# Causal attention in a decoder kernel: the query-side mask moves from TensorE to VectorE

## The chip, the cores and the metric

The kernel runs on one core of one Trainium2 chip. The metric is the time of one execution on the device, in microseconds (us). The time given for a kernel is the median of its runs.

A core has five engines that run side by side, each with its own queue of instructions in order: TensorE (PE in the profile, its weight loads as PEld), VectorE (DVE, here also "the Vector"), ScalarE (ACT), GpSimd (POOL) and SyncE (SP, which here only starts DMAs). They wait for each other through semaphores. TensorE writes its results to PSUM, which here is used as eight banks of 512 float32 per partition; the other engines read them from there.

## The reference

The program is a decoder of four layers on `x` of 8 batches x 256 positions x 256 features. Each layer has a self-attention-like part, a cross-attention-like part and a feed-forward part. Of the twelve parts one has a causal mask, the self-attention of the last layer, and the change concerns only that one:

```
def _L3_attn_ref(x, Wq, bq, Wk, bk, Wv, bv, Wo, bo, Wq_lsr, Wk_lsr):
    N_HEADS = 16;  D_HEAD = 16;  LSR_RANK = 32          # x is (8, 256, 256)
    q = split_heads(x @ Wq.T + bq)
    k = split_heads(x @ Wk.T + bk)
    v = split_heads(x @ Wv.T + bv)
    q_lr = jnp.einsum('bhtd,hdr->bhtr', q, Wq_lsr)
    k_lr = jnp.einsum('bhtd,hdr->bhtr', k, Wk_lsr)
    scores = jnp.einsum('bhir,bhjr->bhij', q_lr, k_lr) / sqrt(LSR_RANK)
    causal_mask = jnp.triu(jnp.ones((Tq, Tq), dtype=bool), k=1)
    scores = jnp.where(causal_mask, -inf, scores)
    attn = softmax(scores, axis=-1)
    y = einsum('bhij,bhjd->bhid', attn, v)
    return merge_heads(y) @ Wo.T + bo
```

So there are 8 x 16 = 128 heads of 256 queries by 256 keys, each with 16 features.

## The kernel before

The parts run one after the other, and each has its own method. The causal part is `l3_attn` (L1708 to L1794). Its core is `attend` (L299), which the three cross-attention parts use too, without the mask.

**Two sets of scores.** A softmax over keys needs, for each query, the largest score to subtract. `attend` computes the scores twice. `score(n, t)` (L336) computes the scores of head n *by query*: partitions are 128 queries, t = 0 or 1 for the two halves, and keys lie along the row. `peak(n)` (L350) takes the negated maximum of each row on the Vector and writes it into one extra column of the query tile `q`. Later `turn` transposes that tile, so that the negated maximum becomes one more feature of the query. `weigh(m, k)` (L367) then computes the scores *by key*: partitions are 128 keys, queries lie along the row, and the extra feature (with a 1 on the key side) subtracts the maximum inside the matmul. `exponentials(m)` (L381) applies exp on ScalarE, and `blend` (L391) multiplies by the values. The by-key scores can be used as a matmul operand without a transpose.

**What the causal mask leaves.** Of the by-query scores the upper half of the queries needs 128 keys (t = 0), the lower half 256 (t = 1). Of the by-key scores the first 128 keys need 256 queries, the second 128 keys need 128. In each, two blocks of 128 x 128 lie on the diagonal, and there the triangle above the diagonal must get -1e30.

**The mask as a matmul.** `masked(bank, cols, which)` (L330) adds the triangle to both diagonal blocks of a bank with one matmul in bfloat16: weights are the identity, `self.tri[:, 0]`, and the moving operand is a triangle of 0 and -1e30, `self.tri[:, 1]` for scores by query and `self.tri[:, 2]` for scores by key (transposed), repeated twice. It accumulates onto the scores that are already in the bank, at line L334 in the profile. `peak` calls it ahead of its two `tensor_reduce` (L359), `exponentials` ahead of its exp (L388).

**The loop and its order.** The loop at L464 goes through slots n, one per head. In slot n it issues score(n, 0), weigh(n - 10, 0), score(n - 1, 1), weigh(n - 11, 1), then peak(n - 1) and exponentials(n - 11), and then whatever other work is due in this slot: projections and keys of the next batch, the transposes of `turn`, `divide` and `blend` after every fourth slot, the output projection, and the next part (`l3_xattn`), which is interleaved as `beside` and `behind`. The four score matmuls of a slot use 17 or 18 of the 128 rows of TensorE, each in another quarter of the rows, so that they can run at the same time; each float32 matmul is two instructions. The order of TensorE and of the Vector is the program's own order (`self.pinned = "both"`); ScalarE and GpSimd may be ordered by the planner. In the first ten slots there is no by-key work yet, in the last ten no by-query work.

**Banks.** Six PSUM banks (`ps_m`) go round between the scores by query, the scores by key and the other matmul results. A score bank becomes free when `peak` has read it, a by-key bank when exp has read it.

`tensor_tensor_reduce`, which the change brings in, already occurs once in this kernel, in the first layer: it shows in the profile as a pair of Vector instructions, `CUSTOM_DVE_ANT_0` (the elementwise operation and running reduction, which also writes its elementwise result, here to a tile that nobody reads) and `DVE_READ_ACCUMULATOR2_ANT` (which writes the reduced column).

Of the kernel before, what the change touches and what calls it, by code (L numbers as in the profile page):

```python
# [21 lines left out]
F32 = mybir.dt.float32  # L22
I32 = mybir.dt.int32
BF16 = mybir.dt.bfloat16
# [3 lines left out]
ALU = mybir.AluOpType  # L28
AX = mybir.AxisListType
PSUM = bass.MemoryType.PSUM  # L30

P = 128
B, S, D = 8, 256, 256
# [5 lines left out]
BIG = 1.0e30  # L39


C_COS, C_SIN, C_DECAY, C_CAUSAL, C_IOTA, C_PIDX, C_HEADS, C_ONE17, C_BEFORE, C_END = (
    0, 256, 512, 1024, 1280, 1536, 1538, 1666, 1667, 1795
)
# [18 lines left out]
class InOrder:  # L63


    def __init__(self, tc, engine):
        self.tc, self.engine = tc, engine
# [10 lines left out]
class Decoder:  # L78
    def __init__(self, ctx, tc, dram, out):
        self.tc, self.nc, self.dram, self.out = tc, tc.nc, dram, out  # L80
        nc = self.nc
        pool = lambda name, bufs, **kw: ctx.enter_context(tc.tile_pool(name=name, bufs=bufs, **kw))
        self.const = pool("const", 1)
        self.res = pool("res", 1)
        self.ring = pool("ring", RING)
        self.small = pool("small", 3)
        self.in_order = [InOrder(tc, e) for e in (nc.tensor, nc.vector, nc.scalar, nc.gpsimd)]
        self.flip = 0
        self.side = "left"

        self.pinned, self.next, self.ready = False, None, None

        self.x = []
        for b in range(B):
            xb = self.res.tile([P, 2, D], F32, tag=f"x{b}", name=f"x{b}")
            nc.sync.dma_start(xb, dram["x"][b].rearrange("(h p) d -> p h d", p=P))
            self.x.append(xb)
        self.xn = self.res.tile([P, NT, D], F32, tag="xn", name="xn")
        self.xnT = self.res.tile([P, 2, N], F32, tag="xnT", name="xnT")

        self.ident = self.const.tile([P, P], F32, tag="ident", name="ident")
        make_identity(nc, self.ident)
        self.ones = self.filled("ones", [P, P], 1.0)
        self.minus = self.filled("minus", [P, 2], -0.5)
        self.eps5 = self.filled("eps5", [P, 1], 1e-5)
        self.junk = self.const.tile([P, 512], F32, tag="junk", name="junk")
        self.cst = self.const.tile([P, C_END], F32, tag="cst", name="cst")
        nc.scalar.dma_start(self.cst, dram["consts"])

        self.tri = self.const.tile([P, 3, P], BF16, tag="tri", name="tri")  # L110
        nc.gpsimd.tensor_copy(self.tri[:, 0, :], self.ident)
        nc.gpsimd.tensor_copy(self.tri[:, 1:3, :].rearrange("p a s -> p (a s)"), self.cst[:, C_CAUSAL : C_CAUSAL + S])

# [183 lines left out]
    def attend(self, pool, nh, dh, prepare, finish, scale=1.0, causal=False, beside=None, behind=None):  # L299
# [14 lines left out]
        nc = self.nc  # L314
# [11 lines left out]
        def rows(n, k):  # L326
            h = n % nh
            return slice(R * (h % hp), R * (h % hp) + k), h // hp

        def masked(bank, cols, which):  # L330

            out = bank.rearrange("p (x s) -> p x s", s=P)[:, 0 : cols // P + 1 : cols // P, :]
            mask = self.tri[:, which : which + 1, :].to_broadcast([P, 2, P])
            self.pe(nc.tensor.matmul(out, lhsT=self.tri[:, 0, :], rhs=mask, start=False, stop=True))  # L334

        def score(n, t):  # L336

            if not 0 <= n < total:
                return
            q, kT, v = state[n // nh]  # L340
            if t == 0:
                ps[n] = self.bank(512)
            r, g = rows(n, dh + 1)
            w = P if causal and t == 0 else S
            self.pe(nc.tensor.matmul(  # L345
                ps[n][:, S * t : S * t + w], lhsT=qTs[n // hp][r, t * P : (t + 1) * P], rhs=kT[r, g, :w],
                start=t == 0 or not causal, stop=not causal,
            ))

        def peak(n):  # L350
            if not 0 <= n < total:
                return
            q = state[n // nh][0]
            to = q[:, :, n % nh, dh + 1]
            bank = ps.pop(n)
            if causal:
                masked(bank, 384, 1)
                for t, cols in ((0, slice(0, P)), (1, slice(S, 512))):
                    self.dve(nc.vector.tensor_reduce(  # L359
                        to[:, t : t + 1], bank[:, cols], axis=AX.X, op=ALU.max, negate=True  # L360
                    ))
            else:
                self.dve(nc.vector.tensor_reduce(  # L363
                    to, bank.rearrange("p (t s) -> p t s", t=2), axis=AX.X, op=ALU.max, negate=True
                ))
# [15 lines left out]
        def exponentials(m):  # L381
            if not 0 <= m < total:
                return
            bank = ps.pop((m, 1))
            if causal:
                masked(bank, 256, 2)
            p = pool.tile([P, n3], F32, tag="p", name="p", bufs=9 if halves else 5)
            nc.scalar.activation(p, bank[:, :n3], AF.Exp, scale=scale)  # L388
            live_p[m] = p
# [74 lines left out]
        while todo or now[0] <= total + lag + 1:  # L464
            n = now[0]
            m = n - lag
            if halves:
                score(n, 0), weigh(m, 0), score(n - 1, 1), weigh(m - 1, 1)
                peak(n - 1), exponentials(m - 1)
            else:  # L470
                score(n, 0), weigh(m, 0), score(n, 1), weigh(m, 1)
                peak(n), exponentials(m)
            for fn in todo.pop(n, ()):
                fn()
            now[0] += 1
# [1232 lines left out]
    def l3_attn(self, pool):  # L1708
# [3 lines left out]
        nc, dram = self.nc, self.dram  # L1712
        w = self.weights(dram["l3a_w"])
# [12 lines left out]
        a = pool.tile([P, 2, P], F32, tag="a", name="a", bufs=1)  # L1726
# [53 lines left out]
        def finish(b, o, later):  # L1780
# [9 lines left out]
            later(4, out)  # L1790
            return 6

        beside, behind = self.l3_xattn(pool)
        self.attend(pool, 16, 16, prepare, finish, 1.0 / math.sqrt(32.0), True, beside, behind)  # L1794

# [332 lines left out]
```

## Time and profile before

| | |
|---|---|
| median of 3 runs | 2464.55 us |
| the 3 runs | 2462.15, 2464.55, 2473.96 us |
| the profiled execution | 2461.47 us |
| its span, first to last instruction | 2459.7 us |
| mean granted TensorE clock over the span | 0.935 |
| the causal stage, from the start of the first mask matmul to that of the last | 2014.6 to 2316.0 us |
| mask matmuls in it (L334) | 256, half of them by query |
| `tensor_reduce` in it (L359) | 256, mean 352 ns |

The profile is one execution; its own time is 3.1 us below the median of the runs, so sums are made against it and then carried to the median. Busy time is given per engine and per group of instructions; the "granted clock" is the share of full speed that the chip's throttle gave to TensorE, 1.00 or 0.50 at any moment. The timeline lists instructions in order of time, with those of one kind that follow each other merged (x2 is two instructions, and the duration is that of both together), and in brackets the idle time ahead of an instruction with what ended it; "issue" there is time in which the engine waited for nothing that the profile shows. A table of windows gives busy time, number of instructions and granted clock of stretches of the span.

### The profile page before, as it was taken

To read this page: it belongs to the slowest core of one execution; us is meant where nothing else is said; L and a number is where in the kernel's file an instruction comes from. 1 tells how busy PE (TensorE), PEld (TensorE's weight loads), DVE (VectorE), ACT (ScalarE), POOL (GpSimd) and SP (SyncE) were. 2 spreads that over 40 slices of the span, in tenths; PEclk is the share of its full clock that TensorE was granted. 3 is DMA by queue.
4 is the path that set the end of the run, shared out by engine and by line. 5 is a ranking of instruction groups with operands and counts; after the bars stand their busy time and mean duration, and the time that the engine had idled before them with its cause. 6 is when DMAs were issued, how large, how long until landed. Compare 5 with 4: busy or idle time off the path is not lost. (4 is left out here: it accounts for less than half of the span.)

```text
span 2459.7 us, 31787 instructions
## 1 busy us (share of the span) xinstructions
PE 2217.8 (90%) x11611; PEld 1410.8 (57%) x11611; DVE 1245.0 (51%) x3192; ACT 872.7 (35%) x2118; POOL 501.0 (20%) x712
## 2 busy tenths in 40 slices
PE   7888889999999999899899955666999989999999
PEld 4555555666655555555568833444665555566556
DVE  5666553334323235676565558985453235555500
ACT  3433422334211113466113335664552114434311
POOL 3211333221000002221135534440222110000010
PEclk9999999999999999899899976886899998899999
DMA  3000000001100000121515643100111010000000
GB/s 128 1 1 1 30 14 26 18 10 41 52 13 26 13 18 13 48 66 36 210 53 165 153 95 104 46 18 14 49 39 32 1 52 10 18 18 18 3 13 22
DMA packets 56539, 103.68 MB, mean 42 GB/s; under 512 B 7624, under 2 KB 40224, under 8 KB 54720
## 3 DMA queue, kind: packets, MB, share of 16 engines
q1 hardware_dynamic: 44688, 75.90, 9.0%
q0 software_dynamic: 7680, 20.98, 3.7%
q10 hardware_dynamic: 4016, 4.76, 0.6%
q8 instruction: 94, 1.54, 0.3%
q14 instruction: 61, 0.50, 0.1%
HBM read 84.64 MB, written 16.78 MB: 41 GB/s over the span
## 5 line engine op out<-in xcount | busy, mean ns | idle before, releaser
L169 PE MATMUL mm<-xnT,w 128*128 128x512 f32 (+1 forms) x1104 | 475.3, 577 | 1.4 <-ACT xnT L252 0.7
L345 PE MATMUL mm<-kT,qT 17*128 17x256 f32 (+2 forms) x1536 | 322.4, 413 | 15.7 <-DVE q L363 12.7
L169 PEld LDWEIGHTS mm<-xnT,w 128*128 128x128 f32 x1104 | 210.6, 193 | 201.2 <-issue 192.1
L376 PE MATMUL mm<-qT,kT 18*128 18x256 f32 (+2 forms) x1536 | 309.5, 406 | 1.4 <-ACT p L388 1.2
L388 ACT ACTIVATE p<-mm 128x512 f32<-128x512 f32 (+1 forms) x384 | 212.1, 562 | 262.0 <-PE mm L376 137.1
L363 DVE TENSOR_REDUCE q<-mm 128x2 f32<-128x512 f32 x256 | 172.3, 688 | 164.1 <-PE mm L376 148.7
L345 PEld LDWEIGHTS mm<-kT,qT 17*128 17x128 f32 (+1 forms) x1536 | 179.1, 193 | 115.0 <-issue 41.3
L560 ACT ACTIVATE hT<-mm 128x512 f32<-128x512 f32 x104 | 62.1, 597 | 431.0 <-PE mm L169 416.6
L561 DVE TENSOR_TENSOR hT<-hT,mm 128x512 f32<-128x512 f32 x104 | 71.4, 687 | 278.2 <-PE mm L169 278.1
L536 PE MATMUL acc<-w,hT 128*128 128x256 f32 x832 | 195.5, 379 | 1.0 <-DVE x L271 1.0
L536 PEld LDWEIGHTS acc<-w,hT 128*128 128x128 f32 x832 | 157.9, 190 | 62.9 <-issue 41.6
L376 PEld LDWEIGHTS mm<-qT,kT 18*128 18x128 f32 (+1 forms) x1536 | 172.3, 191 | 13.2 <-issue 4.6
L235 POOL TENSOR_SCALAR rstd<-mv 128x2 f32<-128x2 f32 x64 | 12.3, 193 | 812.7 <-DVE mv L231 466.8
L399 PE MATMUL acc<-p,v 128*32 128x256 f32 (+2 forms) x1536 | 140.3, 386 | 0.0
L271 DVE TENSOR_TENSOR x<-x,mm 128x512 f32<-128x512 f32 x40 | 27.4, 686 | 193.1 <-PE mm L169 192.9
L297 ACT COPY qT<-tp 128x256 f32<-128x256 f32 x256 | 83.7, 375 | 84.0 <-PE tp L293 83.1
L1290 POOL DMA_INDIRECT xg<-xd,token x96 | 90.9, 947 | 87.8 <-PE tp L1413 54.2
L359 DVE TENSOR_REDUCE q<-mm 128x1 f32<-128x128 f32 (+1 forms) x256 | 78.7, 352 | 56.4 <-PE mm L334 56.1
L169 PE MATMUL mm<-wall,xT 128*128 x384 | 99.7, 383 | 1.1 <-DVE xT L1415 1.1
L293 PE MATMUL tp<-ident,q 128*128 128x128 f32 x512 | 90.6, 299 | 3.3 <-ACT qT L297 1.9
L399 PEld LDWEIGHTS acc<-p,v 128*32 128x32 f32 (+1 forms) x1536 | 61.1, 122 | 47.0 <-issue 21.5
L293 PEld LDWEIGHTS tp<-ident,q 128*128 128x128 f32 x512 | 60.7, 149 | 44.6 <-issue 32.0
(426 smaller groups left out, 3778.8 us busy)
## 6 DMA issues: line engine op xcount, KB each, us to landing
wall<-in_l1f_w SPq DMA_DIRECT2D x8, 1536.0 KB
yd<-y SPq DMA_DIRECT2D x96, 128.0 KB
kT<-in_ctxK SPq DMA_DIRECT2D x16, 512.0 KB
v<-in_ctxV SPq DMA_DIRECT2D x16, 512.0 KB
w<-in_l0f_w SPq DMA_DIRECT2D x8, 768.0 KB
cT<-in_ctxT SPq DMA_DIRECT2D x8, 512.0 KB
ctx<-in_ctx SPq DMA_DIRECT2D x8, 512.0 KB
w<-in_l2f_w SPq DMA_DIRECT2D x3, 768.0 KB
```

Source lines behind the costliest of these rows:

```text
L169: self.pe(self.nc.tensor.matmul(out, lhsT=lhsT, rhs=rhs, start=i == 0, stop=i == len(pairs) - 1))
L293: self.pe(self.nc.tensor.transpose(ps[:, i, t * P : (t + 1) * P], flat[:, t, g * P : (g + 1) * P], self.ident))
L297: self.nc.scalar.copy(dst, ps[:, i, :])
L345: self.pe(nc.tensor.matmul(ps[n][:, S * t : S * t + w], lhsT=qTs[n // hp][r, t * P : (t + 1) * P], rhs=kT[r, g, :w], start=t == 0 or not c ...
L359: self.dve(nc.vector.tensor_reduce(to[:, t : t + 1], bank[:, cols], axis=AX.X, op=ALU.max, negate=True))
L363: self.dve(nc.vector.tensor_reduce(to, bank.rearrange("p (t s) -> p t s", t=2), axis=AX.X, op=ALU.max, negate=True))
L376: self.pe(nc.tensor.matmul(ps[m, 1][:, 256 * k : 256 * k + w], lhsT=kT[r, g, k * P : (k + 1) * P], rhs=qTs[m // hp][r, S - w :], start=k = ...
L388: nc.scalar.activation(p, bank[:, :n3], AF.Exp, scale=scale)
L399: self.pe(nc.tensor.matmul(acc[r, S - w :], lhsT=v[:, k, (G * hp + i) % nh, :], rhs=live_p[G * hp + i][:, 256 * k : 256 * k + w], start=k ...
L536: self.pe(nc.tensor.matmul(acc[:, t, :], lhsT=hT[:, t * P : (t + 1) * P], rhs=units[i][2], start=i == 0 and t % 2 == 0, stop=i == len(unit ...
L561: nc.vector.tensor_tensor(hT, hT, u, ALU.mult)
L1290: (engine or self.nc.gpsimd).indirect_dma_start(out=dst, out_offset=None, in_=src, in_offset=bass.IndirectOffsetOnAxis(ap=rows, axis=0))
```

## The change

Scores by query are no longer masked on TensorE. `peak` instead calls `tensor_tensor_reduce` on the Vector for each half: it adds a tile `self.later` (0 for the first 128 keys where there are 256, then the triangle of 0 and -1e30) to the scores from PSUM, scales by -1, writes the result to a tile `self.void` that nobody reads, and takes the minimum along the row, starting from 1e30, which is the negated maximum. Scores by key keep their mask matmul, so `masked` loses its arguments and the triangle by query leaves `self.tri`. The score matmuls now each start and stop their own result (`start=True, stop=True`), since nothing is accumulated onto them. Two tiles of 1 KB per partition are set up once ahead of the part.

```
-        self.tri = self.const.tile([P, 3, P], BF16, tag="tri", name="tri")
+        self.tri = self.const.tile([P, 2, P], BF16, tag="tri", name="tri")
         nc.gpsimd.tensor_copy(self.tri[:, 0, :], self.ident)
-        nc.gpsimd.tensor_copy(self.tri[:, 1:3, :].rearrange("p a s -> p (a s)"), self.cst[:, C_CAUSAL : C_CAUSAL + S])
+        nc.gpsimd.tensor_copy(self.tri[:, 1, :], self.cst[:, C_CAUSAL + P : C_CAUSAL + S])
...
-        def masked(bank, cols, which):
+        def masked(bank):
-            out = bank.rearrange("p (x s) -> p x s", s=P)[:, 0 : cols // P + 1 : cols // P, :]
-            mask = self.tri[:, which : which + 1, :].to_broadcast([P, 2, P])
+            out = bank.rearrange("p (x s) -> p x s", s=P)[:, 0:3:2, :]
+            mask = self.tri[:, 1:2, :].to_broadcast([P, 2, P])
             self.pe(nc.tensor.matmul(out, lhsT=self.tri[:, 0, :], rhs=mask, start=False, stop=True))
...
-                start=t == 0 or not causal, stop=not causal,
+                start=True, stop=True,
...
             if causal:
-                masked(bank, 384, 1)
-                for t, cols in ((0, slice(0, P)), (1, slice(S, 512))):
-                    self.dve(nc.vector.tensor_reduce(
-                        to[:, t : t + 1], bank[:, cols], axis=AX.X, op=ALU.max, negate=True
-                    ))
+                for t, w in ((0, P), (1, S)):
+                    self.dve(nc.vector.tensor_tensor_reduce(
+                        out=self.void[:, :w], in0=bank[:, S * t : S * t + w], in1=self.later[:, S - w :], scale=-1.0,
+                        scalar=BIG, op0=ALU.add, op1=ALU.min, accum_out=to[:, t : t + 1],
+                    ))
...
-                masked(bank, 256, 2)
+                masked(bank)
...
+        self.void = pool.tile([P, S], F32, tag="void", name="void", bufs=1)
+        self.later = pool.tile([P, S], F32, tag="later", name="later", bufs=1)
+        nc.vector.memset(self.later[:, :P], 0.0)
+        nc.vector.tensor_copy(self.later[:, P:], self.cst[:, C_CAUSAL : C_CAUSAL + P])
         beside, behind = self.l3_xattn(pool)
         self.attend(pool, 16, 16, prepare, finish, 1.0 / math.sqrt(32.0), True, beside, behind)
```

## The prediction

> **What bounds the kernel now.** I read the page first, then the stage from the first mask matmul to the last (2014.4 to 2316.6) in the table of windows, then its groups of instructions by form.
>
> ```profile
> PE 2217.8 (90%) x11611; PEld 1410.8 (57%) x11611; DVE 1245.0 (51%) x3192; ACT 872.7 (35%) x2118; POOL 501.0 (20%) x712
> ...
> PEclk9999999999999999899899976886899998899999
> ```
> ```profile
> 2014.40:2316.60 302.20, 299.14 (x2421) 179.26 (x2422) 163.30 (x514) 122.38 (x293) 16.80 (x38) 0.95 0.05 15
> ```
>
> In the stage TensorE is busy 299.14 of 302.20 us, the Vector 163.30 (54%). The stage is as long as TensorE's queue. So what comes off that queue comes off the time, and work added to the Vector costs nothing until it delays TensorE. The clock is not full: 0.95 here, and two of the fortieths in the stage (2029 to 2152) show 8.
>
> ```profile
> L359 DVE TENSOR_REDUCE q<-mm 128x1 f32<-128x256 f32 x124 | 51.4, 415 | 0.0
> L334 PE MATMUL mm<-tri 128*128 128x256 bf16 x241 | 50.0, 289 | 0.0
> ...
> L359 DVE TENSOR_REDUCE q<-mm 128x1 f32<-128x128 f32 x124 | 35.9, 289 | 50.5 <-PE mm L334 50.3
> ```
>
> These groups (2020 to 2300) give a mask 289 ns, but matmuls overlap; what one adds to the queue is read from the timeline, a slot with both masks first, then one of the first ten, which has one:
>
> ```profile
> 2150.39 0.11 PEld L334 LDWEIGHTS <-tri 128*128 128x128 bf16 x2 [0.33 <-issue]
> ...
> 2150.72 0.18 PEld L345 LDWEIGHTS mm<-kT,qT 17*128 17x128 f32 x1 [0.21 <-issue]
> 2150.72 0.62 DVE L359 TENSOR_REDUCE q<-mm 128x1 f32<-128x128 f32 x2 [0.46 <-PE mm L334]
> ...
> 2151.05 0.37 PE L345 MATMUL mm<-kT,qT 17*128 17x256 f32 x1
> ...
> 2151.36 0.11 PEld L334 LDWEIGHTS <-tri 128*128 128x128 bf16 x2 [0.33 <-issue]
> ```
> ```profile
> 2017.20 0.10 PEld L334 LDWEIGHTS <-tri 128*128 128x128 bf16 x1 [0.33 <-issue]
> 2017.42 0.30 PEld L345 LDWEIGHTS mm<-kT,qT 17*128 17x128 f32 x4
> ```
>
> From the masks to the next score matmul it takes 2150.72 - 2150.39 = 0.33 us with two, 2017.42 - 2017.20 = 0.22 with one. A mask costs 0.107 us of the queue at full clock. The 0.33 us ahead of the masks stands in both cases, and stays as long as one mask is left.
>
> **The clock follows the work in the array.** The windows decide this case. Cutting the span into 3.41 us windows (the length of the shortest low stretch in the clock's record; all others are multiples), the clock is 1.00 or 0.50 for whole windows:
>
> ```profile
> 2098.11:2101.53 3.42, 3.25 (x31) 1.45 (x28) 2.76 (x9) 1.27 (x4) 0.89 (x2) 1.00 0.00 0
> 2101.53:2104.94 3.41, 3.41 (x16) 2.15 (x16) 1.61 (x6) 1.18 (x3) 0.00 (x0) 0.50 0.01 2
> ...
> 2255.13:2258.54 3.41, 3.24 (x39) 1.67 (x38) 3.06 (x10) 1.83 (x6) 0.88 (x2) 1.00 0.82 255
> 2258.54:2261.95 3.41, 3.41 (x36) 2.20 (x38) 2.75 (x10) 2.03 (x5) 0.00 (x0) 1.00 0.13 55
> ```
>
> Both first windows have TensorE busy 3.25 us; after one the clock is halved, after the other not. What differs is how much of the array works. I define a window's load as the sum over its matmul instructions of streaming time at full clock x rows x columns / (128 x 128), divided by 3.41 us. A float32 instruction streams 128 columns in 0.107 us (those of 512 columns follow each other after 0.43), a mask its 256 bfloat16 columns in 0.107. So a mask is 0.107 / 3.41 = 0.031. A slot's scores are eight instructions, 2 x (0.107 + 0.213 + 0.213 + 0.107) = 1.28 us, on 17.5 of 128 rows: 0.051. Four transposes are 0.125, a blend (32 of 128 columns) 0.19. The window from 2098.11 holds 2.6 slots and six masks: 0.32, low clock follows. That from 2255.13 holds a blend, two slots, 3.65 masks and a bit: 0.43, full clock follows. Over all 663 windows whose widths the trace gives, the load of a window told the clock of the next: below 0.375, half in 92 of 94; above, full in 568 of 569. TensorE's idle time is not what counts: the masks, full-array work, hold the clock up.
>
> **The change part by part.** *Masks by query, removed:* 128 x 0.107 = 13.7 us off the queue. In about four of the first ten slots no full-array work remains between two groups of scores, and the switch of up to 0.55 us goes too: at most 4 x 0.44 = 1.8 more, which I put at nothing, since these windows lose load as well.
>
> *The same masks, as load:* a stretch of slots alone, before, has a period of 0.96 us: 3.41 / 0.963 x (0.051 + 2 x 0.031) = 0.40, above 0.375. After, the period is 0.856: 3.41 / 0.856 x (0.051 + 0.031) = 0.33, below it. At half clock such a stretch is worth half, so the clock stays low until transposes, blends or projections fill a window. Taking the first mask of each pair out of the windows as they stand, those from 2070.81 (0.39 to 0.29), 2180.03 and 2255.13 (both 0.43 to 0.37) fall below, and four others come within 0.025; before there were three, from 2029.85, 2063.98 and 2098.11, with 9 low windows, 30.7 us, which cost half of that, 15.4. Where windows begin in the program is not fixed (the three runs spread over 12 us), so I moved the window border through 100 positions over TensorE's own order of the stage, low stretches brought to full speed, and applied the 0.375. Before: 2.3 falls, 33 us low, 16.6 lost. After, with 0.107 us taken out per mask: 6.8 falls, 87 us low, 43.5 lost; 49.4 if each slot also stalls 15 ns on the Vector. I take 46.5. Tenth and ninetieth per cent without stalls are 20 and 65. Against 16.6 that is +29.9, from +4 to +48.
>
> *Rule against row:* the Trainium skill, "TensorE: Matmul & The Clock Gate", section "HAM oscillation", says that the clock falls back when TensorE has idle gaps longer than about 3.4 us. In the low window from 2101.53, and in the one ahead of it, TensorE is busy 3.41 and 3.25 us. By that rule the clock term would be 0 and the sum -11.4 us; by the row it is +18.5.
>
> *Reductions become add-and-minimum:* the nearest rows are the same operation in the first layer:
>
> ```profile
> 63.36 0.43 DVE L71 CUSTOM_DVE_ANT_0 void<-e,u 128x256 f32<-128x256 f32 x1
> 63.71 0.08 DVE L71 DVE_READ_ACCUMULATOR2_ANT cm<- 128x1 f32 x1
> 63.91 0.16 DVE L71 SCALAR_TENSOR_TENSOR cb<-cm,ca 128x1 f32<-128x1 f32 x1
> ```
>
> 256 columns take 0.43 us, as the reduction does; the read starts 0.35 after and takes 0.08; the next starts 0.55 after, but needs the result. By the reductions 128 columns are 0.126 shorter. A pair is then 0.30 + 0.43 = 0.73 us, 0.62 if reads hide, 0.97 with 0.55 each; now 0.62. I take 0.73, the same operation without the dependence: 128 x 0.11 = 14 us (0 to 45) on the Vector, 54% to 59% busy. What hides it: the score matmul that ends last, from 2151.05 for 0.37, is done at 2151.42, 0.06 after the masks' start, so the pair starts at about 0.10 instead of 0.33. It ends at 0.83, at worst 1.07, and the bank is wanted back by the second next group, 0.22 + 0.86 = 1.08 after the masks (two slots of both before: 0.95 against 1.29). Behind it on the Vector wait only the later parts of the same slots. Cover is gone where the Vector is full already, 8.10 of 10 us from 2180 and 9.21 from 2280: about 8 slots x 0.11 each, 2 us together. At 0.97 it would be up to 128 x 0.11 = 14.
>
> *Setup and the rest:* a fill and a copy of 128 columns ahead of `l3_xattn` on the Vector: a 128x256 operation from SBUF is 0.29 us, so at most 0.6, while the Vector is busy 8.47 of 20 us there; 0.3. The shorter copy on GpSimd, `start`/`stop`, and the order of queues: nothing moves; 0.
>
> **Sum.** -13.7 + 29.9 + 2.3 = +18.5. From the median, 2464.55, that is 2483; from the profiled execution (2461.47, 15.4 lost), 2461.47 - 13.7 + 31.1 + 2.3 = 2481.2. Forecast 2482.
>
> **Rivals.**
> *The clock does not follow* (faster or the same): the load was only a companion of something else, perhaps of real idleness. Then -13.7 + 2.3: 2453, and 2451 with the first slots' switches; it decides if the falls stay at three. For it: l1_xattn runs slots without masks at 1.00 from 1019 to 1100. Against it: its score matmuls are all 256 wide and none of its windows there lies below 0.375; and the rule holds in 660 of 663.
> *Luck with the borders*: the batch's period falls from 37.8 us, about 11 windows, to 36, so borders drift through the batch; if only four falls come, at 43.5 / 6.8 = 6.4 us each, 26 are lost, 9 more than before: 2464.55 - 13.7 + 9 + 2.3 = 2462.
> *The Vector becomes the bound*: the pair costs 0.97, beyond the new slot's 0.856: +14 of stalls, which thin the load further (by 15 ns a slot the loss rose 6): 2464.55 - 13.7 + 14 + 33 = 2498. Against it: the 0.55 contains a wait for the result.
>
> **How the numbers follow.** The measurement can tell about 0.5%, 12.3 us. The forecast has 0.62 (0.50 of it beyond 2477, 0.12 below), the deaf clock 0.13 (0.06 below 2452, 0.07 within), luck 0.13 (0.02 below, 0.09 within, 0.02 beyond), the Vector 0.12. Faster 0.08, same 0.28, slower 0.64. The range goes from 2453, which leaves out most of the deaf clock's lower half, to 2499; within the forecast alone it is 2466 to 2497.
>
> **What would show it.** Masks at L334: 128 instead of 256, slots 0.107 us closer at full clock. Right: five or more falls of the clock in the stage, some 60 to 110 us at half clock (before 30.7), mean granted clock of the stage near 0.85, windows of slots alone at load 0.33 ahead of them. Vector pairs at 0.73 us, few TensorE waits for `q`. Wrong: slots closer and the clock at 0.95, or long TensorE waits for the Vector.

## The result, and the profile after

The changed kernel takes 2474.9 us, median of 13 runs (2469.57 to 2491.1), against 2465.78 for the kernel before in the same comparison (13 runs, 2459.58 to 2480.33). The ratio is 1.0041, 95% interval 1.0021 to 1.0061: slower by 10 us (5 to 15). The forecast was 2482 in a range of 2453 to 2499, so the sign and the range held; the loss is about half of what the sum said, and lies within the half per cent on which the prediction had put 0.28. In what follows one run, of the kernel called the addition alone, was in a slower state (2654.9 us, its others 2461 to 2477); it counts in that kernel's median and in no ratio.

The profiled execution took 2476.95 us, against 2461.47 before. Its page gives the engines' busy time and the granted clock in forty slices:

```profile
PE 2228.6 (90%) x11483; PEld 1413.5 (57%) x11483; DVE 1258.8 (51%) x3450; ACT 873.3 (35%) x2118; POOL 501.1 (20%) x712
...
PEclk9999999999999999899899977776999988887999
```

TensorE has 128 instructions fewer and is busy 10.8 us longer. In the second line the late run of 9s has turned into 8s and a 7: that is the causal stage. The table of windows for the stage, from the start of its first score matmul to that of its last mask (columns: window; its length, then busy time and instructions of TensorE, its weight loads, the Vector, ScalarE, GpSimd; granted clock; DMA share; GB/s):

```profile
2013.82:2332.59 318.77, 310.32 (x2293) 184.23 (x2292) 176.26 (x769) 123.13 (x293) 16.80 (x38) 0.87 0.05 14
```

The same stretch before:

```profile
2013.79:2316.00 302.21, 299.15 (x2421) 179.36 (x2420) 163.24 (x513) 122.25 (x293) 16.80 (x38) 0.95 0.05 15
```

The stage before took 302.21 us with TensorE idle for 3.06 of them and the clock at 0.95. After, it is 16.6 us longer, with 318.77 - 310.32 = 8.45 us idle, at 0.87. In the record of the clock the low stretches of the stage go from three (10.2, 3.4, 17.1 us; 30.7 together) to seven (13.7, 3.4, 3.4, 17.1, 17.1, 17.1, 13.7; 85.3 together). The execution as a whole is 15.5 us longer, so outside the stage it changed by -1.1.

The new Vector work, in the groups of instructions by form (2036 to 2316; busy us, mean ns, idle ahead):

```profile
L359 DVE CUSTOM_DVE_ANT_0 void<-mm,later 128x256 f32<-128x256 f32 x114 | 48.4, 425 | 4.0
...
L334 PE MATMUL mm<-tri 128*128 128x256 bf16 x114 | 35.3, 310 | 0.0
L359 DVE CUSTOM_DVE_ANT_0 void<-mm,later 128x128 f32<-128x128 f32 x114 | 32.8, 288 | 37.3 <-PE mm L345 32.5
...
L359 DVE DVE_READ_ACCUMULATOR2_ANT q<- 128x1 f32 x228 | 18.9, 83 | 0.0
```

and in the timeline, from one mask to the next, a slot without other work at full clock:

```profile
2163.00 0.10 PEld L334 LDWEIGHTS <-tri 128*128 128x128 bf16 x1 [0.33 <-issue]
...
2163.26 0.26 DVE L359 CUSTOM_DVE_ANT_0 void<-mm,later 128x128 f32<-128x128 f32 x1
...
2163.45 0.08 DVE L359 DVE_READ_ACCUMULATOR2_ANT q<- 128x1 f32 x1
...
2163.56 0.42 DVE L359 CUSTOM_DVE_ANT_0 void<-mm,later 128x256 f32<-128x256 f32 x1
...
2163.86 0.10 PEld L334 LDWEIGHTS <-tri 128*128 128x128 bf16 x1 [0.33 <-issue]
...
2163.91 0.08 DVE L359 DVE_READ_ACCUMULATOR2_ANT q<- 128x1 f32 x1
```

From one mask to the next it is 0.86 us, where it was 0.96 with two masks: the slot got shorter by what a mask costs. The Vector's pair goes from 2163.26 to 2163.99, 0.73 us. Both are as the prediction had them. The same view at half clock shows what a slot costs there:

```profile
2234.23 0.10 PEld L334 LDWEIGHTS <-tri 128*128 128x128 bf16 x1 [0.64 <-issue]
2235.72 0.10 PEld L334 LDWEIGHTS <-tri 128*128 128x128 bf16 x1 [0.64 <-issue]
```

That is 1.49 us, 1.74 times 0.854 (the median at full clock), not twice. Over 14 such slots the median is 1.487, so a microsecond at half clock loses 1 - 0.854 / 1.487 = 0.43 us; by the slots with two masks before, 1 - 0.962 / 1.700 = 0.43 as well. The prediction took 0.50.

Three windows of 3.41 us from the table of windows, the first two at full clock, the third following the second:

```profile
2142.51:2145.93 3.42, 3.25 (x42) 1.89 (x34) 3.25 (x13) 1.87 (x6) 0.88 (x2) 1.00 0.01 2
...
2224.43:2227.85 3.42, 3.25 (x35) 1.80 (x31) 3.25 (x13) 1.87 (x5) 0.88 (x2) 1.00 0.02 5
2227.85:2231.26 3.41, 3.41 (x17) 2.32 (x16) 2.40 (x14) 1.01 (x3) 0.00 (x0) 0.50 0.00 0
```

The first two have the same busy time on every engine to within a tenth, and TensorE is busy 3.25 us in both. By the load (streaming time x rows x columns of every matmul, worked out as in the prediction) the first is at 0.386 and the clock stays full after it; the second is at 0.341, and the third is at half clock.

### The profile page after: what moved, and what is told of

The parts are those of the page before. It is cut to its first block, busy times and chain, and to the rows that moved or that the text cites. A ratio compares the mean times of both kernels' runs of the same rounds, so it can differ in the third digit from the quotient of the medians.

```text
span 2474.0 us, 31852 instructions
## 1 busy us (share of the span) xinstructions
PE 2228.6 (90%) x11483; PEld 1413.5 (57%) x11483; DVE 1258.8 (51%) x3450; ACT 873.3 (35%) x2118; POOL 501.1 (20%) x712
## 5 line engine op out<-in xcount | busy, mean ns | idle before, releaser
L345 PE MATMUL mm<-kT,qT 17*128 17x256 f32 (+2 forms) x1536 | 331.8, 422 | 16.4 <-DVE q L364 12.7
L377 PE MATMUL mm<-qT,kT 18*128 18x256 f32 (+2 forms) x1536 | 318.4, 416 | 3.6 <-DVE q L359 2.1
L359 DVE CUSTOM_DVE_ANT_0 void<-mm,later 128x128 f32<-128x128 f32 (+1 forms) x256 | 91.2, 356 | 50.4 <-PE mm L345 40.6
```

Of the source, the lines that this page charges most:

```text
L345: self.pe(nc.tensor.matmul(ps[n][:, S * t : S * t + w], lhsT=qTs[n // hp][r, t * P : (t + 1) * P], rhs=kT[r, g, :w], start=True, stop=True,))
L359: self.dve(nc.vector.tensor_tensor_reduce(out=self.void[:, :w], in0=bank[:, S * t : S * t + w], in1=self.later[:, S - w :], scale=-1.0, sc ...
L377: self.pe(nc.tensor.matmul(ps[m, 1][:, 256 * k : 256 * k + w], lhsT=kT[r, g, k * P : (k + 1) * P], rhs=qTs[m // hp][r, S - w :], start=k = ...
```

## The experiments

Each was compared with the kernel before on the same chip, in three groups. The kernel before took 2462.03 us beside the first four (removal, addition, by-key scores over 32 rows), 2469.86 beside the four with whole groups of rows, and 2462.64 beside the other two, so only ratios are set against each other; a difference in us is the difference of ratios times the time of before. "Load theory" in the expectations is the prediction's: a window below a load of 0.375 is followed by half clock. A "fall" is a change from full to half clock.

Every run, profiled or not, has its mean granted clock on record. Since the clock is 1.00 or 0.50, a run's time at half clock over its whole span is 2 x (1 - clock) x span: 320 us for the profiled execution before, 376 for that of the changed kernel. The mean over runs is 328, 330 and 335 us for the kernel before in the three groups (77 runs, 331 together), and 369 us for the changed kernel (13 runs). So the two profiled executions lie 56 us apart, the kernels only 38.

**The removal alone.** The mask by query is gone and the two `tensor_reduce` stay, so this kernel leaves the causal mask out of the maximum. A copy on ScalarE adds 1e-5, so that no denominator is zero. Against the changed kernel:

```
-                for t, w in ((0, P), (1, S)):
-                    self.dve(nc.vector.tensor_tensor_reduce(
...
+                for t, cols in ((0, slice(0, P)), (1, slice(S, 512))):
+                    self.dve(nc.vector.tensor_reduce(
+                        to[:, t : t + 1], bank[:, cols], axis=AX.X, op=ALU.max, negate=True
                     ))
...
-            nc.scalar.copy(oT, acc)
+            if causal:
+                nc.scalar.activation(oT, acc, AF.Identity, bias=self.eps5)
+            else:
+                nc.scalar.copy(oT, acc)
...
```

> The removal alone: the masks by query are gone from TensorE, and the Vector reduces the unmasked scores with tensor_reduce as before, so the causal mask by query is left out of the maximum; the blend's copy adds 1e-5 so that no denominator is zero. Load theory (the clock of a 3.41 us window follows the array load of the window before, limit 0.375): TensorE's order is that of the changed kernel, so 6 to 8 falls of the clock in the stage, 70 to 90 us at half clock, and 2468 to 2476 us, no faster than before. Vector theory (the time of the changed kernel is the add-and-minimum's): no falls beyond the 2 to 3 of before, 13.7 us faster, 2452.

2472.26 us (2457.97 to 2490.97), ratio 1.0026 (1.0006 to 1.0046): 6 us slower (1 to 11), with 128 matmuls less and nothing added but the 1e-5 (ScalarE is busy 126.07 us in the stage, 122.25 before). Its stage:

```profile
2018.56:2343.76 325.20, 318.61 (x2292) 188.47 (x2292) 161.83 (x513) 126.07 (x293) 16.73 (x38) 0.84 0.05 14
```

105.8 us of it at half clock. (This profile is of the slowest of its runs; over all twelve, half clock over the span is 48 us more than before.) The theory that the Vector's new operations make the change slow falls: without them it is slow too.

**The addition alone.** The Vector's new operation, with both masks left on TensorE.

> The addition alone: masks by query stay on TensorE as before, and the Vector does the add-and-minimum instead of tensor_reduce (the mask is added twice, which changes no maximum). Load theory: load and falls as before (2 to 3 falls, 20 to 35 us at half clock); what is left is the Vector's own price, 0 to 4 us: 2466 to 2470. Vector theory: the Vector's price is the 9 us by which the change is slower plus the 13.7 of the masks, some 23: 2488.

2471.45 us, ratio 1.0030 (1.0011 to 1.0049): 7 us (3 to 12), more than the 0 to 4 that the load theory allowed, though the interval reaches into them, and far from the 23 of the other.

```profile
2012.71:2318.15 305.44, 300.21 (x2420) 178.97 (x2419) 177.74 (x769) 122.34 (x293) 16.81 (x38) 0.95 0.05 15
```

The profiled stage is 3.2 us longer than before, at the same 30.7 us of half clock: some 25 ns a slot, two thirds of it TensorE's idle time (5.2 us against 3.1). Moving the window border over this kernel's own order gives 4.2 falls and 49 us low where before gives 2.3 and 31. By the granted clocks the nine runs have 334 us at half clock against 328 before: 6 more, not 18. At the 0.43 us that one costs (above) that is 2.5, and with the 3.2 of the stage 5.7 of the 7.

**By-key scores over 32 rows,** the rows added holding zeros; streaming time is unchanged.

```
-            r, g = rows(m, dh + 2)
+            r, g = rows(m, 32 if causal else dh + 2)
```

In the changed kernel:

> The changed kernel, but the scores by key contract over 32 rows instead of 18; the 14 more are zero on both sides, so no value changes, and by columns no matmul gets longer. Load theory: a slot's scores weigh 0.072 of a window instead of 0.051, a stretch of slots alone 0.41 instead of 0.33; going through the changed kernel's own order gives 3.6 falls and 41 us at half clock instead of 6.7 and 82, so about 20 us less: 2454 to 2460. Idle theory (the clock falls where TensorE has gaps): nothing changes, 2475.

In the kernel before:

> The kernel before, with the same 32 rows for the scores by key. Load theory: falls go from 2.3 to 1.2, half-clock time from 31 to 18 us, so about 7 us less than before: 2457 to 2461. Idle theory: nothing changes, 2466.

After: 2463.16 us, ratio 0.9990 (0.9975 to 1.0005), so 12.6 us less than the changed kernel as it was. Before: 2449.59 us, ratio 0.9946 (0.9928 to 0.9964), 13.3 us less. The stages:

```profile
2010.57:2312.32 301.75, 292.05 (x2293) 174.65 (x2292) 175.96 (x769) 122.36 (x293) 16.74 (x38) 0.93 0.05 15
```
```profile
2007.08:2295.78 288.70, 285.54 (x2420) 172.83 (x2419) 163.12 (x513) 121.78 (x293) 16.73 (x38) 1.00 0.05 16
```

With 44.4 and 0.0 us at half clock. TensorE does nothing more that is useful and nothing less, and its idle time is that of the kernels with 18 rows: 9.7 us against 8.45, and 3.2 against 3.06. What changed is the number of rows that the matmuls name, and with it the load: half clock over all runs is 8 us more than before in the changed kernel (38 with 18 rows), and 33 less in the kernel before. "Nothing changes", the expectation of the idle theory, is out in both. The load theory had the sign and not the sizes: some 20 us for the first, where it is 12.6 (6 to 19), and 7 for the second, where it is 13.3 (9 to 18).

**Half the dose:** 25 rows, in the changed kernel.

> After, with scores by key read over 25 rows instead of 18, the added ones zero: half the dose of the run with 32 rows, load of a stretch of slots up by 0.014 instead of 0.027. Load theory: between after and the 32 rows, whose difference was some 12 us: 4 to 8 us faster than after, 2467 to 2471 at a before of 2464, with 66 us low in the stage by the moved borders (after 82, 32 rows 41). Rival, only whole groups of 32 rows count (the array switched on by quadrants): as after, 2473 to 2475, and windows whose load by rows and columns is above 0.375 are followed by half clock.

2462.35 us, ratio 1.0008 (0.9989 to 1.0028): 8 us (1 to 15) below the changed kernel, between 18 and 32 rows. The profiled stage has 51.2 us at half clock (18 rows 85.3, 32 rows 44.4); over all runs half clock is 18 us more than before, where 18 rows have 38 and 32 rows 8. That speaks against the rival that only whole groups of 32 rows count, which wanted this kernel like the changed one. All 17 windows of load below 0.375 are followed by half clock, all 77 above by full. The windows alone are thin evidence here, since counting 18 rows for the 25 puts no more than a few of them on the wrong side.

**The matmuls given back.** The mask by key is issued twice in the changed kernel.

```
-                masked(bank)
+                masked(bank, False), masked(bank, True)
```

The argument is the matmul's `stop`.

> After, with the mask by key issued twice into its bank (a second mask over the first changes no exponential: what is masked is already zero). TensorE gets 128 full-array matmuls back, 13.7 us of queue at full clock, the Vector keeps its new operations. Load theory: a stretch of slots is at 0.40 again instead of 0.33, falls go from some 7 back to 2 to 4; the queue grows by 9 to 14 and 15 to 20 us of half clock are saved, so it is no slower than after, about 4 us faster and like the addition alone (before + 7; 2466 to 2473 at a before of 2464). Rival, the time is the queue's length and the Vector's waits: after plus 9 to 14, 2484 to 2489.

2467.74 us, ratio 1.0020 (1.0002 to 1.0038), 5 us below the changed kernel; the two intervals together leave anything from 12 below to 1 above.

```profile
2015.70:2320.00 304.30, 299.17 (x2420) 178.58 (x2420) 176.31 (x769) 122.17 (x293) 16.74 (x38) 0.95 0.05 15
```

With 128 useless matmuls the profiled stage is 14.5 us shorter than the changed kernel's, with 30.7 us at half clock instead of 85.3; over all runs half clock is 11 us more than before, where the changed kernel has 38. The rival, that the length of the queue decides, wanted 9 to 14 us more and is out.

**All four with whole groups of rows,** 31 for scores by query (the 32nd holds the maximum) and 32 by key, to take the clock out of it as far as this goes.

```
-            r, g = rows(n, dh + 1)                 # score
+            r, g = rows(n, 31 if causal else dh + 1)
-            to = q[:, :, n % nh, dh + 1]           # peak
+            to = q[:, :, n % nh, 31 if causal else dh + 1]
-            r, g = rows(m, dh + 2)                 # weigh
+            r, g = rows(m, 32 if causal else dh + 2)
-    c[:, C_ONE17] = np.arange(P) % 32 == 17
+    c[:, C_ONE17] = np.arange(P) % 32 == 31
```

> Before, with the causal scores read over whole groups of rows: scores by query over 31 rows instead of 17, by key over 32 instead of 18; the rows added hold zeros, and the column of the negated maximum moves from 17 to 31. Streaming times stay, the load of a stretch of slots rises from 0.40 to about 0.49. Load theory: moving the window border over the order of before gives 0.3 falls and 2 us low in the stage instead of 2.3 and 31: 15 us less than before, about 2450. Rival, the clock follows TensorE's idleness: nothing changes for it, 2464.

> After, with the same whole groups of rows. Load of a stretch of slots from 0.33 to about 0.43, above 0.375 by 0.05. Load theory: 2.1 falls and 17 us low in the stage (after: 6.7 and 82), and what is left of the change is its queue: 13.7 of masks less about 3 of waits for the Vector, less some 7 for the falls that are left: 3 us below the kernel before with whole rows (2447; 2443 to 2451), 28 below after. So the change turns from a loss of 9 us into a small gain. Rival, idleness: as after, 2475, 11 above the other. Rival, the Vector is what eats the masks' 13.7: as slow as before with whole rows or slower, 2450 to 2460.

> The removal alone (mask by query left out of the computation, reductions as before), with whole groups of rows. Load theory: 1.7 falls, 13 us low; stage 9 us below that of before with whole rows, 13.7 off the queue less what the falls left cost: 2440 (2436 to 2445). If the removed masks were worth nothing by themselves: as before with whole rows, 2450. Its distance to the changed kernel with whole rows is the Vector's price without the clock: 3 to 6 by the 3.8 us that the two stages differ at full clock, 14 if each of 128 pairs delays TensorE by its 0.11.

> The addition alone (the Vector adds and takes the minimum, both masks stay on TensorE), with whole groups of rows. Without them it was 7 us above before, while its stage is only 3.2 longer at full clock. Theory: waits for the Vector of about 3 us, the rest falls of the clock that they bring on. With whole rows the load is 0.48 and 0.6 falls are left: 3 to 4 above the kernel before with whole rows, 2453 to 2454. If all 7 are the Vector's: 2457 or more.

Measured: before 2454.02 us, ratio 0.9945 (0.9923 to 0.9967); changed 2458.07, 0.9958 (0.9942 to 0.9974); removal alone 2444.55, 0.9906 (0.9880 to 0.9932); addition alone 2460.46, 0.9955 (0.9936 to 0.9974). Their stages in this order:

```profile
2018.11:2306.88 288.77, 285.58 (x2420) 172.85 (x2420) 163.22 (x513) 121.77 (x293) 16.74 (x38) 1.00 0.05 16
```
```profile
2025.70:2314.11 288.41, 278.43 (x2292) 168.78 (x2291) 175.85 (x769) 122.10 (x293) 16.80 (x38) 0.98 0.05 16
```
```profile
2028.83:2318.07 289.24, 282.37 (x2293) 170.42 (x2292) 161.82 (x513) 125.63 (x293) 16.80 (x38) 0.96 0.05 16
```
```profile
2022.40:2317.63 295.23, 289.84 (x2420) 174.27 (x2420) 177.50 (x769) 121.86 (x293) 16.74 (x38) 0.99 0.05 16
```

Half clock: 0.0, 13.7, 23.5 and 6.8 us. The first expectation held (13.6 us less than before). The last, 3 to 4 above the first, isn't decided: by the ratios it is 2.5, by the medians 6.4, and the interval holds the rival's 7 as well. The changed kernel did not come out 3 us below before with whole rows but 3 above, with intervals that overlap: the small gain isn't there. The clock is not out of this one: its runs have 26 us more at half clock than those of before with whole rows, 11 us of time at 0.43, which takes back the 6.4 that its queue is shorter. The removal alone is 9.6 us (1 to 18) below the first, as expected, though its profile (the slowest of its seven runs) shows none of it: its stage has the most half clock of the four.

That the waits grow is seen in TensorE's idle time, length less busy: 3.2 us before, 10.0 changed, 6.9 removal, 5.4 addition. What TensorE waited for in the first two (us, times, longest):

```profile
PE mm L169 <- ACT p L388: 1.2, 4, 0.3
PE mm L376 <- ACT p L388: 1.2, 7, 0.2
PE mm L376 <- DVE q L359: 0.4, 2, 0.2
PE mm L345 <- DVE q L359: 0.3, 1, 0.3
```
```profile
PE mm L169 <- ACT p L389: 4.2, 5, 1.0
PE mm L377 <- DVE q L359: 3.4, 8, 0.6
PE mm L377 <- ACT p L389: 1.2, 7, 0.2
PE mm L345 <- DVE q L359: 1.0, 1, 1.0
```

Waits for the Vector's maxima grow by 3.7 us, and those of projections for a bank that exp holds by 3.0. A faster slot meets the same two engines sooner.

**All kernels in one table.** In the profiled executions, the stage's length less 0.43 times its time at half clock should be the length of the queue at full clock, and the same for kernels that differ in rows alone:

| kernel | stage, us | at half clock | at full clock |
|---|---|---|---|
| before | 302.21 | 30.7 | 289.0 |
| before, 32 rows by key | 288.70 | 0 | 288.7 |
| before, whole rows | 288.77 | 0 | 288.8 |
| addition alone | 305.44 | 30.7 | 292.2 |
| addition, whole rows | 295.23 | 6.8 | 292.3 |
| changed, mask by key twice | 304.30 | 30.7 | 291.1 |
| removal alone | 325.20 | 105.8 | 279.7 |
| removal, whole rows | 289.24 | 23.5 | 279.1 |
| changed | 318.77 | 85.3 | 282.1 |
| changed, 25 rows by key | 304.43 | 51.2 | 282.4 |
| changed, 32 rows by key | 301.75 | 44.4 | 282.7 |
| changed, whole rows | 288.41 | 13.7 | 282.5 |

It is, to 0.6 us; with 0.50 in place of 0.43 the four changed kernels would be 5.4 us apart. So the masks by query are worth 9.4 us of queue, the Vector's operation costs 3.0 to 3.4, the change as a whole is about -6.5, and the rest of what any of these profiles shows in the stage is the clock.

The same sum can be set against the times of all runs, with the half clock of every run from its granted clock. The last two columns are in us against the kernel before of the same group (for the changed kernel, whose own comparison has no clocks for before, the half clock is against all 77 runs):

| kernel | queue | half clock, more | queue + 0.43 x half clock | measured (95%) |
|---|---|---|---|---|
| changed | -6.4 | 38 | 9.8 | 10.1 (5.2 to 15.0) |
| removal alone | -9.4 | 48 | 11.2 | 6.4 (1.5 to 11.3) |
| addition alone | 3.4 | 6 | 5.9 | 7.4 (2.7 to 12.1) |
| changed, 32 rows by key | -6.4 | 8 | -2.8 | -2.5 (-6.2 to 1.2) |
| before, 32 rows by key | 0 | -33 | -14.0 | -13.3 (-17.7 to -8.9) |
| changed, 25 rows by key | -6.4 | 18 | 1.5 | 2.0 (-2.7 to 6.9) |
| changed, mask by key twice | 2.3 | 11 | 6.9 | 4.9 (0.5 to 9.4) |
| before, whole rows | 0 | -37 | -16.0 | -13.6 (-19.0 to -8.2) |
| changed, whole rows | -6.4 | -12 | -11.4 | -10.4 (-14.3 to -6.4) |
| removal, whole rows | -9.4 | -30 | -22.3 | -23.2 (-29.6 to -16.8) |
| addition, whole rows | 3.4 | -34 | -11.3 | -11.1 (-15.8 to -6.4) |

All eleven agree within their intervals. The price comes out of the runs too: within the runs of one kernel, 194 in all, the time rises by 0.44 us (0.40 to 0.47) for each us at half clock.

In the twelve profiles the windows around the stage number 1127: of 142 below a load of 0.375, 139 are followed by half clock, and the three others are at 0.371, 0.373 and 0.374; all 985 above are followed by full clock. This is by the prediction's working; with every matmul placed by its recorded start, or by its end, 8 or 13 of 1089 windows miss, all between 0.34 and 0.40. So the limit is known to a few hundredths.

## Why the prediction was partly right

*The queue, -13.7: the step that failed is "what comes off that queue comes off the time".* A slot is shorter by the 0.107 us of a mask, as said. But with the masks gone TensorE idles 3.7 us more (removal, whole rows: 6.9 against 3.2), and 13.7 - 3.7 = 10.0 is near the 9.4 of the table (which also holds the change of `start` and `stop` and the 1e-5 of the removal; no run parts them). The prediction counted no wait that would be late next once the queue is shorter; it is the exponentials' bank and the maxima.

*The Vector, +2.3:* 3.0 to 3.4. Pairs at 0.73 us, few waits, cover mostly there. The rival "the Vector becomes the bound" is out: 14 us of stalls were wanted for it, and the addition alone has 3.4 at full clock.

*The clock, +29.9: the mechanism was right, the size was off.* Falls in the profile were 7 for 6.8, time at half clock 85.3 us for 87; that it came so near is in part luck, since this execution has 376 us at half clock over its span and the mean run 369. The first error is the price: not every part of a slot doubles (the mask's weight load takes 0.10 us at both clocks), so that low time costs 0.43 of itself, not half. In the profiled pair of executions that is (85.3 - 30.7) x 0.43 = 23.5, and -6.9 + 23.5 = 16.6 us is the stage's whole difference. The Trainium skill, "TensorE: Matmul & The Clock Gate", section "HAM oscillation", reckons throttled time at half its length too; the slots here, 0.854 and 1.487 us, give 0.43.

The second error is the amount. 10 us slower with 6.5 off the queue leaves 16 to 17 for the clock (12 to 22 by the interval), which is 36 to 40 us more at half clock, where the profiles have 55 and the moved borders had 54. The granted clocks of the runs say 38. So the profiled pair was further apart than the kernels are (before at 320 us where its runs have 331, the changed kernel at 376 where they have 369), and borders moved evenly over one execution's order gave 16 us too many. Why they do stays open. With both errors put right, 38 x 0.43 = 16 in place of 29.9, and -6.4 + 16 = 10 is the measured loss.

*The rule against the row:* by idle gaps of more than 3.4 us the sum was -11.4. The runs say +10, and adding rows of zeros, which leaves TensorE's idle time within 1.3 us, takes 12.6 us off. "The clock does not follow" is out by both.

*Luck with the borders* had 2462 with four falls. The profile had seven, and over the runs half clock is 38 us more, where four falls would have added 18 (4 x 87 / 6.8 - 33); but the spread is real: the removal alone ran from 2458 to 2491 us, before with whole rows from 2451.5 to 2460.

*The windows named* did fall: that from 2070.81 is at 0.328 in the changed kernel (2070.84), that from 2180.03 at 0.341 (2180.06). The one from 2255.13 had moved; falls came after 2224.43 and 2268.81 instead.

The best version needs no change of the masks: before, with its causal score matmuls read over 32 rows by key, or over whole groups in both, at 0.9946 and 0.9945 of the time, one line or four.

## What to carry to other kernels

Where matmuls use few rows of the array, look at the clock before taking full-array work away: here 128 masks that took 9.4 us of the queue also held the clock up, and without them it took back more (16 us for the 6.4 that the change as a whole took off the queue). Work out the load of windows of one clock period, see which stretches are near the border in the clock's record, and try first to use more rows at no streaming time (zeros will do). And price a cut in the queue of the bounding engine with the wait that comes next, not by its own length.

## What the runs showed of the hardware that was not expected

Rows that hold zeros count as load: reading 32 rows instead of 18 in the by-key scores took the stage from 30.7 us at half clock to none, and 13.3 us off the time. 128 full-array matmuls added without use, 8.7 us of queue by the table, made the changed kernel no slower (5 us faster, between 12 faster and 1 slower), since its runs lost 27 us at half clock by them. Half clock costs 0.43 of its duration in these slots, 0.854 us becoming 1.487, and 0.44 over the runs. And the mean granted clock of a run, which needs no profile, tells its time at half clock well enough to account for the times of eleven kernels.
